# Two cross-attention layers on one core: the second layer's queries in two banks, and queries and keys dealt out anew over the steps

## The chip, the core and the metric

The kernel runs on one NeuronCore of a Trainium2 chip. The core has TensorE (PE in the profile; its weight loads are PEld), VectorE (DVE), ScalarE (ACT), GpSimd (POOL) and SyncE (SP), which only issues DMA transfers here. The metric is the device time of one execution in microseconds (us). Each engine takes its instructions strictly in the order in which the program lists them; an instruction whose operand or buffer is not ready holds up everything behind it on its engine.

## The reference

Input are 64 batches of 256 positions with 320 channels (x), and for each batch 77 context rows of 512 values (73 of text, 4 of an image in the second layer). Both layers have 20 heads of 16 channels. All is float32.

```python
# layer 0: the text path over all 77 rows
q = x @ Wq.T; k = ctx @ Wk.T; v = ctx @ Wv.T          # split into 20 heads
x = softmax(q k^T / 4) v  @ Wo.T + bo + x
# layer 1: 73 text rows, and 4 image rows
q = x @ W_q; k = text @ W_k; v = text @ W_v
probs = softmax(q k^T / 4);  text_out = probs v
qsem = l2norm(probs @ text)                             # 512 values for each head and position
sem = qsem . l2norm(ip)
probs_ip = softmax(q k_ip^T / 4 + 0.5 * sem) * spatial_mask
x = (text_out + probs_ip v_ip) @ W_out + b_out + x
```

In layer 0 the reference's context is cut after 77 rows, so its own image part is over an empty set of rows and adds nothing.

## The kernel before

The kernel keeps channels on the partitions and positions on the free axis. It works on pairs of batches (p = 0 to 31), so that 512 positions are in hand at a time. The 320 channels are held as 2 x 128 ("main") and a rest of 64 ("last"); the rest is stored with batch 0 of the pair on partitions 0 to 63 and batch 1 on partitions 64 to 127.

The attention of one layer and one batch is cut into five units (`UNITS`): two groups of 8 heads times two halves of 128 positions, and one unit with the last 4 heads of both halves. A pair has NU = 10 units. The main loop (line 1050) runs over units g; k = g % 10 is the unit's place in the pair. In step g the kernel handles unit g of layer 0 and unit g - 13 of layer 1, so layer 1 of a pair runs about one pair behind layer 0. A step issues, in this order:

1. `early` and `drains`: what was held from the step before, among it the second part of a projection made in two banks (`held`).
2. on TensorE into the four-bank tile "sc" (one buffer): the `semantics` matmuls of an earlier layer-1 unit (L744, L750), then the scores of both layers (L641).
3. `shifted` on VectorE: maximum and subtraction for each layer (L659, L661).
4. `transposed(1)`: five transposes of layer 1 (L705, L706) into two "tr" tiles, copied out by ScalarE (L712, L713).
5. the exponential of layer 0 on ScalarE (L669), and `weighted` on VectorE (L761, L764).
6. the fillers of the list `first`.
7. `transposed(0)`: the same transposes for layer 0, into two more "tr" tiles, copied out by ScalarE (L731, L732 or L720, L723).
8. the copy of the sums out of "sc" (L1096), the exponential of layer 1 (L672, L673), `normalize` (VectorE L687, L688, POOL L692) and a VectorE reduction (L1107).
9. the fillers of `second`; after the unit u = 1 or u = 4 of layer 0 the attention over the values (`attend`, L777, L782, copied by L801); then the fillers of `third`.

Since "sc" has one buffer, the next step's semantics wait for L1096 of this step, which waits for VectorE. PSUM has two more kinds of tile of a bank each: "tr" with two buffers and "ms" with two. Every filler that multiplies takes "ms" tiles in turn, and its first matmul waits until the tile two before it in the program has been copied out.

The fillers are dealt out by hand, by k, in the function `fillers` (line 941): projections, queries, keys, values, gram matrices and their placements. `keep_order` (line 46) fixes the order of TensorE, ScalarE, VectorE and POOL as the program gives it.

The change touches these fillers: `queries(l, p, m)` makes 128 query channels (m = 0 or 1) of both batches in one bank: two matmuls over 512 columns for the main channels, and two over 256 columns for the last 64 contracted channels, with weights padded by zeros to 128 rows (`wq[l][:, 2 + b]`). For m = 2 it makes the last 64 query channels. `first_queries(p)` makes the first 256 query channels of layer 0 through `halves`: each batch has a bank of its own, eight matmuls over 256 columns for the main channels, and four with only 64 rows for the last channels, one per batch on its own half of the rows. `halves` also serves the output projections `project`. `keys(l, p, i)` makes 128 key channels, `keys_by_head` spreads them by head on POOL.

Layer 1's queries read x after layer 0's `project` and `project_last` have added their results to it (L601, L620 on VectorE).

Of the kernel before, what the change touches and what calls it, by code (L numbers as in the profile page):

```python
# [8 lines left out]
F32 = mybir.dt.float32  # L9
# [9 lines left out]
S = 256  # L19
# [3 lines left out]
P = 128  # L23
# [40 lines left out]
def tile_two_cross_attentions(ctx: ExitStack, tc: tile.TileContext, a: dict, out: bass.AP):  # L64
# [35 lines left out]
    nc = tc.nc  # L100
# [3 lines left out]
    S2 = 2 * S  # L104

    const = ctx.enter_context(tc.tile_pool(name="const", bufs=1))
    big = ctx.enter_context(tc.tile_pool(name="big", bufs=2))
# [5 lines left out]
    pms = ctx.enter_context(tc.tile_pool(name="pms", bufs=2, space=PSUM))  # L113
# [36 lines left out]
    cts, xts = {}, {}  # L150
# [20 lines left out]
    wv, wq, wo, bo = [None] * 2, [None] * 2, [None] * 2, [None] * 2  # L171
# [152 lines left out]
    kTs, kbds, qs, vips, aTs = {}, {}, {}, {}, {}  # L324
# [195 lines left out]
    def halves(name, w, src):  # L520


        main, last = src
        ps = [pms.tile([P, 2, S], F32, tag="ms", name=f"{name}_{b}") for b in range(2)]
        for b in range(2):
            for k in range(2):
                for m in range(2):
                    nc.tensor.matmul(  # L528
                        ps[b][:, m, :], w[:, k, m * P : (m + 1) * P], main[:, k, b * S : (b + 1) * S],
                        start=(k == 0 and m == 0), stop=False,  # L530
                    )

        def rest():
            for m in range(2):
                for b in range(2):
                    rows = slice(b * HALF, (b + 1) * HALF)
                    nc.tensor.matmul(  # L537
                        ps[b][:, m, :], w[rows, 2 + b, m * P : (m + 1) * P], last[rows, :],
                        start=False, stop=(m == 1),
                    )  # L540
            return ps

        return rest

    held = {}

    def queries(l, p, m):

        main, last = xts[p]
        ps = pms.tile([P, 512], F32, tag="ms", name=f"q_ps{l}_{p}_{m}")  # L550
        if m < 2:
            q = qs[l, p, m] = big.tile([P, S2], F32, tag=f"q{l}{m}", name=f"q{l}_{p}_{m}", bufs=1)
            c = slice(m * P, (m + 1) * P)
            for i in range(2):
                nc.tensor.matmul(ps, wq[l][:, i, c], main[:, i, :], start=(i == 0), stop=False)  # L555
            for b in range(2):
                nc.tensor.matmul(ps[:, b * S : (b + 1) * S], wq[l][:, 2 + b, c], last, start=False, stop=(b == 1))  # L557
            nc.scalar.copy(q, ps)
            return
        to = [ps[s * HALF : (s + 1) * HALF, :S].rearrange("p (b t) -> p b t", b=2) for s in range(2)]  # L560
        for i in range(2):
            for s in range(2):
                nc.tensor.matmul(  # L563
                    to[s], wq[l][:, i, C - HALF :],
                    main[:, i, :].rearrange("p (b s t) -> p b s t", b=2, s=2)[:, :, s, :],
                    start=(i == 0), stop=False,
                )
        for b in range(2):
            for s in range(2):
                nc.tensor.matmul(  # L570
                    to[s][:, b, :], wq[l][:, 2 + b, C - HALF :], last[:, s * P : (s + 1) * P],
                    start=False, stop=(b == 1),
                )
        q = qs[l, p, 2] = big.tile([P, 2, P], F32, tag=f"q{l}2", name=f"q{l}_{p}_2", bufs=1)
        nc.scalar.copy(q.rearrange("p b t -> p (b t)"), ps[:, :S])

    def first_queries(p):

        rest = halves(f"q_ps0_{p}", wq[0], xts[p])

        def end():
            ps = rest()
            q = big.tile([P, 2, S2], F32, tag="q0", name=f"q0_{p}")
            for m in range(2):
                qs[0, p, m] = q[:, m, :]
            return [lambda b=b: nc.scalar.copy(q[:, :, b * S : (b + 1) * S], ps[b]) for b in range(2)]  # L586

        held["q"] = end

    def project(l, p):  # L590

# [349 lines left out]
    def fillers(k, p):  # L941


        f = ([], [], [], [])

        def add(half, q, fn, *args):
            if 0 <= q < NP:
                f[half].append((fn, args))

        if k == 0:  # L950
            if p == 0:
                for l in range(2):
                    add(0, p, value_rows, 0, l)
                add(1, p, values, 0, p, 0)
            add(0, p - 1, gram, p - 1, 0)
            add(0, p - 3, project_last, 1, p - 3)
            add(2, p - 2, text_transposed, p - 2, 0)
            if p:
                add(2, p, place_values, 0, p, 0)
            add(2, p - 1, values, 1, p - 1, 0)  # L960
        elif k == 1:
            if p == 0:
                for l in range(2):
                    add(l, p, value_rows, 1, l)
                add(1, p, place_values, 0, p, 0)
            add(0, p, queries, 0, p, 2)
            add(1, p - 1, project, 0, p - 1)
            add(1, p - 1, place_gram, 0)
            add(1, p, keys_by_head, 0, p, 1)
            add(1, p - 1, keys_by_head, 1, p - 1, 0)  # L970
        elif k == 2:
            if p == 0:
                for i in range(2):
                    add(0, p, keys, 1, p, i)
            add(0, p - 1, project_last, 0, p - 1)
            add(1, p + 1, load_x, p + 1)
            add(1, p - 1, queries, 1, p - 1, 0)
            add(1, p - 1, place_values, 1, p - 1, 0)
            add(1, p, values, 0, p, 1)
        elif k == 3:  # L980
            add(0, p + 1, load_context, p + 1)
            add(0, p - 1, queries, 1, p - 1, 2)
            if p == 0:
                add(1, p, image_keys, 0)
            add(1, p - 1, queries, 1, p - 1, 1)
            add(1, p, place_values, 0, p, 1)
            add(1, p - 1, keys_by_head, 1, p - 1, 1)
        elif k == 4:
            if p == 0:
                add(0, p, image_keys, 1)  # L990
            else:
                add(0, p, keys, 1, p, 0)
            add(1, p - 1, values, 1, p - 1, 1)
            add(1, p + 1, first_queries, p + 1)
        elif k == 5:
            if p == 0:
                add(0, p, image_keys, 2)
            add(0, p + 1, keys, 0, p + 1, 0)
            add(2, p - 2, text_transposed, p - 2, 1)
        elif k == 6:  # L1000
            while len(made_rows) * P < min(NB, 2 * (p + 2)) * T:
                rows_todo.extend((len(made_rows), l) for l in range(2))
                made_rows.append(rows_todo[-1])
            for n in range(len(rows_todo) // 2):
                add(0, p, value_rows, *rows_todo.pop(0))
            if p == 0:
                add(0, p, image_norms)
            else:
                add(1, p, keys, 1, p, 1)
            add(1, p - 1, gram, p - 1, 1)  # L1010
            add(1, p, place_image_keys, p)
        elif k == 7:
            add(0, p + 1, keys, 0, p + 1, 1)
            add(1, p + 1, last_keys, p + 1)
            add(1, p - 2, lambda: made.update(wT=image_transposed(p - 2)))
            add(1, p - 1, place_values, 1, p - 1, 1)
            add(1, p - 1, image_values, p - 1, 0)
            if p == 0:
                add(1, p, image_rows)
        elif k == 8:  # L1020
            while rows_todo:
                add(0, p, value_rows, *rows_todo.pop(0))
            add(1, p - 1, place_gram, 1)
            add(1, p + 1, keys_by_head, 0, p + 1, 0)
            add(1, p - 1, image_values, p - 1, 1)
            add(1, p - 2, image_attend_last, p - 2)
            add(3, p - 2, lambda: held.update(i=lambda: image_attend(p - 2)))
        else:
            add(0, p - 2, project, 1, p - 2)
            add(1, p + 1, values, 0, p + 1, 0)  # L1030
            for b in range(2):
                add(1, p - 1, place_image_values, p - 1, b)
        return f
# [7 lines left out]
        keys(0, 0, i)  # L1041
    last_keys(0)
    keys_by_head(0, 0, 0)
    first_queries(0)
    for fn in held.pop("q")():
        fn()

# [2 lines left out]
    for g in range(NP * NU + LAG + 12):  # L1050
        p, k = divmod(g, NU)
# [5 lines left out]
        ps = prod = None  # L1057
# [3 lines left out]
        if now[0] or now[1] or before1:  # L1061
            ps = psc.tile([P, 4, 512], F32, tag="sc", name=f"sc{g}")
# [42 lines left out]
        if before1:  # L1105
            q, b, u = before1[:3]
# [9 lines left out]
        if last0:  # L1116
            q, b, u, _ = last0
# [60 lines left out]
```

## Time and profile before

| | |
|---|---|
| median of 3 runs | 2630.31 us (2629.02 to 2631.37) |
| profiled execution | 2628.61 us, its span 2626.9 us |
| PE busy | 2549.2 us, 97% of the span |
| DVE busy | 1969.9 us, 75% |
| ACT busy | 1538.8 us, 59% |
| POOL busy | 1442.4 us, 55% |
| mean granted TensorE clock | 0.986 |
| unit k = 0 to 9 of one steady pair (from 1249.97 us on) | 8.07, 9.40, 8.62, 7.45, 8.69, 6.43, 6.94, 6.95, 7.51, 7.81 us |
| the pair | 77.87 us |

A float32 matmul of the program stands in the trace as two MATMUL instructions, so a count of x16 is eight matmuls. The end of a matmul is modelled, and the next one of the same kind begins before it; for the time that a group takes, the start of the next group minus its own start is used below. In a timeline a line holds start, duration, engine, line of the program, operation, tiles, tile shape, count, and in brackets the engine's idle time before it and the last of what it waited for.

### The profile page before, as it was taken

The page shows a single profiled execution, that of the slowest core. Times are in us where ns is not written, and L with a number is a line of the kernel's source. Part 1 is how long each engine was busy: PE and PEld are TensorE (multiplying, and loading weights), DVE is VectorE, ACT ScalarE, POOL GpSimd, SP SyncE. Part 2 cuts the span into 40 slices and gives each one's busy share as a digit, 9 for nine tenths or more (in the row PEclk, how much of TensorE's full clock was granted, in tenths as well). Part 3 has the DMA queues.
Part 4 walks back from the last instruction along what each step waited for, and adds up shares of the span by engine and source line. Part 5 has one row for each costly group of instructions (what it writes and reads, how often), then busy time and mean ns, then how long its engine had stood idle before and what let it go on. Part 6 is the DMA issues. An engine that isn't in the chain of part 4 may idle for free.

```text
span 2626.9 us, 73603 instructions
## 1 busy us (share of the span) xinstructions
PE 2549.2 (97%) x26792; PEld 1974.0 (75%) x26792; DVE 1969.9 (75%) x3639; ACT 1538.8 (59%) x3991; POOL 1442.4 (55%) x3515
## 2 busy tenths in 40 slices
PE   7999999999999999999999999999999999999897
PEld 5677777777777777777777777777777777777675
DVE  3577777777777777777777777777777777777864
ACT  3465665655665665665665665655665655665643
POOL 2455555565555565555565555565555565555542
PEclk9999999999999999999999999999999999999986
DMA  5212211112111112111112111112111112111000
GB/s 163 72 29 58 58 42 47 42 51 57 57 44 47 42 51 58 58 42 48 42 52 57 58 42 48 41 52 58 58 42 48 41 52 58 56 38 36 26 22 23
DMA packets 154657, 132.24 MB, mean 50 GB/s; under 512 B 48249, under 2 KB 132985, under 8 KB 154297
## 3 DMA queue, kind: packets, MB, share of 16 engines
q1 hardware_dynamic: 153432, 126.38, 16.8%
q8 instruction: 215, 3.52, 0.5%
q10 hardware_dynamic: 864, 1.15, 0.1%
q14 instruction: 146, 1.19, 0.1%
HBM read 89.53 MB, written 33.91 MB: 47 GB/s over the span
## 4 chain that ended last, share of the span: by engine, by line
PE 87%; DVE 6%; ACT 3%; DMA 1%; issue 1%; POOL 1%; SPq 0%; POOLq 0%; DVEq 0%; ACTq 0%
PE sc L744 13%; PE tr L705 11%; PE o_ps L528 8%; PE sc L641 7%; PE v_ps L379 6%; PE sc L750 5%; PE q_ps L555 4%; PE q_ps L528 4%; PE k_ps L334 4%; PE o_ps L616 3%; PE o_ps L537 3%; PE pv L777 2%; DVE w L661 2%; PE q_ps L557 2%; PE q_ps L563 2%; PE rtr L706 2%
## 5 line engine op out<-in xcount | busy, mean ns | idle before, releaser
L659 DVE TENSOR_REDUCE mx<-sc 128x8 f32<-128x584 f32 (+1 forms) x640 | 497.6, 778 | 460.1 <-PE sc L641 460.0
L692 POOL TENSOR_TENSOR parts<-w,sm 128x512 f32<-128x512 f32 (+1 forms) x640 | 439.6, 708 | 301.6 <-ACT parts L673 180.7
L661 DVE TENSOR_TENSOR w<-sc,mx 128x616 f32<-128x616 f32 x640 | 511.9, 800 | 66.7 <-DVE mx L659 0.5
L712 ACT COPY pt<-tr 128x512 f32<-128x512 f32 x320 | 186.8, 584 | 449.3 <-PE tr L705 437.5
L705 PE MATMUL tr<-ident,parts 128*128 128x128 f32 x2560 | 412.8, 284 | 12.8 <-POOL parts L692 5.2
L744 PEld LDWEIGHTS sc<-gv,pt 64*128 64x128 f32 x5120 | 323.5, 191 | 117.2 <-ACT sums L1096 67.5
L744 PE MATMUL sc<-gv,pt 64*128 64x94 f32 x5120 | 363.3, 282 | 35.1 <-ACT sums L1096 32.7
L705 PEld LDWEIGHTS tr<-ident,parts 128*128 128x128 f32 x2560 | 284.5, 142 | 124.6 <-issue 88.8
L676 POOL COPY att<-w 128x32 f32<-128x32 f32 x320 | 66.8, 209 | 469.7 <-DVE w L661 469.0
L669 ACT ACTIVATE w<-w 128x616 f32<-128x616 f32 x320 | 232.0, 725 | 96.3 <-DVE w L661 95.4
L687 DVE TENSOR_REDUCE sm<-w 128x8 f32<-128x616 f32 x320 | 248.2, 776 | 13.5 <-ACT w L669 13.5
L641 PE MATMUL sc<-kbd,q 32*128 32x154 f32 x5120 | 250.0, 308 | 1.0 <-ACT q L586 0.8
L528 PE MATMUL o_ps<-aT,wo 128*128 128x256 f32 x1024 | 234.3, 383 | 1.6 <-POOL aT L923 1.6
L1107 DVE TENSOR_REDUCE nrm<-prod 128x8 f32<-128x584 f32 x320 | 227.4, 711 | 0.4
L761 DVE TENSOR_TENSOR prod<-sc,parts 128x512 f32<-128x512 f32 x320 | 218.0, 681 | 5.5 <-PE sc L750 5.5
L528 PEld LDWEIGHTS o_ps<-aT,wo 128*128 128x128 f32 x1024 | 192.0, 193 | 25.8 <-POOL aT L923 2.4
L672 ACT ACTIVATE parts<-w 128x512 f32<-128x512 f32 x320 | 206.8, 646 | 0.0
L641 PEld LDWEIGHTS sc<-kbd,q 32*128 32x128 f32 x5120 | 188.5, 188 | 6.0 <-issue 5.0
L731 ACT COPY pt<-tr 128x512 f32<-128x512 f32 x256 | 150.6, 588 | 67.5 <-PE tr L705 66.8
L379 PE MATMUL v_ps<-wv,cf 128*128 128x320 f32 (+1 forms) x624 | 182.1, 438 | 0.0
L706 PE MATMUL rtr<-ident,parts 128*104 128x128 f32 (+1 forms) x640 | 175.9, 275 | 0.0
L1096 ACT COPY sums<-sc 128x168 f32<-128x168 f32 x320 | 96.6, 302 | 118.9 <-DVE prod L764 118.0
(148 smaller groups left out, 4802.9 us busy)
## 6 DMA issues: line engine op xcount, KB each, us to landing
vip<-vip_rows SPq DMA_DIRECT2D x1280, 5.0 KB
out_dram<-x SPq DMA_DIRECT2D x64, 256.0 KB
x<-in_x_dram SPq DMA_DIRECT2D x31, 512.0 KB
v_rows<-vs SPq DMA_DIRECT2D x38, 320.0 KB
vm<-v_rows SPq DMA_DIRECT2D x152, 80.0 KB
ct<-in_ctx_dram SPq DMA_DIRECT2D x32, 308.0 KB
cf<-in_ctx_dram SPq DMA_DIRECT2D x38, 256.0 KB
g_rest<-gram_rest SPq DMA_DIRECT2D x512, 0.5 KB
```

Of the source, the lines that this page charges most:

```text
L379: nc.tensor.matmul(ps[:n, :C], cfs[i][:, k, :n], wv[l][:, k, :], start=(k == 0), stop=(k == KE - 1))
L528: nc.tensor.matmul(ps[b][:, m, :], w[:, k, m * P : (m + 1) * P], main[:, k, b * S : (b + 1) * S], start=(k == 0 and m == 0), stop=False,)
L641: nc.tensor.matmul(ps[:, r, 2 * T * l : 2 * T * (l + 1)], q[rows, b, :] if part == 2 else q[rows, t0 : t0 + P], kbd[rows, part].rearrange( ...
L659: nc.vector.tensor_reduce(mx, sc[:, :, :, :nt], AX.X, ALU.max)
L661: nc.vector.tensor_tensor(w, sc, mx.unsqueeze(3).broadcast_to([P, 4, 2, T]), ALU.subtract)
L669: nc.scalar.activation(w, w, AF.Exp, scale=SCALE)
L687: nc.vector.tensor_reduce(sm, w, AX.X, ALU.add)
L692: nc.gpsimd.tensor_tensor(two[:, 8 * t0 : 8 * t1].rearrange("p (h t) -> p h t", h=8), w[:, :, t0:t1], sm.unsqueeze(2).broadcast_to([P, 8, ...
L705: nc.tensor.transpose(ps[:, i, :], flat[:, i * P : (i + 1) * P], ident)
L706: nc.tensor.transpose(pr[:n, 0, :], flat[:, 4 * P : 4 * P + n], ident)
L744: nc.tensor.matmul(ps[:, i % 2 * 2 + j, at : at + GV], pt[half_rows, i, :], gv[b][half_rows, part, i, :], start=start and i < 2, stop=False,)
L1107: nc.vector.tensor_reduce(eight(stats[q, b][2], u), prod, AX.X, ALU.add)
```

## The change

`first_queries` becomes `queries(l, p)` for both layers. The first 256 query channels of layer 1 are now made by `halves` too: a batch in each of two "ms" banks, the last contracted channels as two row tiles of 64 rows. In layer 0 the second part is still held over to the next step; in layer 1 the second part and the two copies follow at once. The tile of layer 1's queries is one tile "q1" with one buffer instead of two tiles. The last 64 query channels keep their form, in a function of their own, `last_queries`.

The fillers are dealt out anew:

- the last queries of layer 0: from k = 1, first list, to k = 3, second list
- the first 256 queries of layer 1: from k = 2 and k = 3 (a half in the second list of each) to k = 2, third list, that is after the attention
- `keys_by_head` of layer 1, batch 1: from k = 3 to k = 2, second list, ahead of `place_values`
- the first half of layer 1's keys (p > 0): from k = 4, first list, to k = 3, second list

```diff
-    def queries(l, p, m):
+    def last_queries(l, p):
 
         main, last = xts[p]
-        ps = pms.tile([P, 512], F32, tag="ms", name=f"q_ps{l}_{p}_{m}")
-        if m < 2:
-            q = qs[l, p, m] = big.tile([P, S2], F32, tag=f"q{l}{m}", name=f"q{l}_{p}_{m}", bufs=1)
-            c = slice(m * P, (m + 1) * P)
-            for i in range(2):
-                nc.tensor.matmul(ps, wq[l][:, i, c], main[:, i, :], start=(i == 0), stop=False)
-            for b in range(2):
-                nc.tensor.matmul(ps[:, b * S : (b + 1) * S], wq[l][:, 2 + b, c], last, start=False, stop=(b == 1))
-            nc.scalar.copy(q, ps)
-            return
+        ps = pms.tile([P, 512], F32, tag="ms", name=f"q_ps{l}_{p}_2")
...
-    def first_queries(p):
+    def queries(l, p):
 
-        rest = halves(f"q_ps0_{p}", wq[0], xts[p])
+        rest = halves(f"q_ps{l}_{p}", wq[l], xts[p])
 
         def end():
             ps = rest()
-            q = big.tile([P, 2, S2], F32, tag="q0", name=f"q0_{p}")
+            q = big.tile([P, 2, S2], F32, tag=f"q{l}", name=f"q{l}_{p}", bufs=2 - l)
             for m in range(2):
-                qs[0, p, m] = q[:, m, :]
+                qs[l, p, m] = q[:, m, :]
             return [lambda b=b: nc.scalar.copy(q[:, :, b * S : (b + 1) * S], ps[b]) for b in range(2)]
 
-        held["q"] = end
+        if l:
+            for fn in end():
+                fn()
+        else:
+            held["q"] = end
...
         elif k == 1:
...
-            add(0, p, queries, 0, p, 2)
             add(1, p - 1, project, 0, p - 1)
...
         elif k == 2:
...
-            add(1, p - 1, queries, 1, p - 1, 0)
+            add(1, p - 1, keys_by_head, 1, p - 1, 1)
             add(1, p - 1, place_values, 1, p - 1, 0)
             add(1, p, values, 0, p, 1)
+            add(2, p - 1, queries, 1, p - 1)
         elif k == 3:
             add(0, p + 1, load_context, p + 1)
-            add(0, p - 1, queries, 1, p - 1, 2)
+            add(0, p - 1, last_queries, 1, p - 1)
             if p == 0:
                 add(1, p, image_keys, 0)
-            add(1, p - 1, queries, 1, p - 1, 1)
+            if p:
+                add(1, p, keys, 1, p, 0)
+            add(1, p, last_queries, 0, p)
             add(1, p, place_values, 0, p, 1)
-            add(1, p - 1, keys_by_head, 1, p - 1, 1)
         elif k == 4:
             if p == 0:
                 add(0, p, image_keys, 1)
-            else:
-                add(0, p, keys, 1, p, 0)
             add(1, p - 1, values, 1, p - 1, 1)
-            add(1, p + 1, first_queries, p + 1)
+            add(1, p + 1, queries, 0, p + 1)
```

More of the change, by code (lines that the diff above doesn't have):

```diff
@@ L1043, in tile_two_cross_attentions @@
     keys_by_head(0, 0, 0)
-    first_queries(0)
+    queries(0, 0)
     for fn in held.pop("q")():
```

## The prediction

> **What bounds the kernel now.** I read the page's busy shares first, then the timeline of one steady pair (units g = 160 to 165), cut into its units by the first semantic matmul (L744) of each, then places where the trace already shows what the change will make. The page's first part:
>
> ```profile
> PE 2549.2 (97%) x26792; PEld 1974.0 (75%) x26792; DVE 1969.9 (75%) x3639; ACT 1538.8 (59%) x3991; POOL 1442.4 (55%) x3515
> ```
>
> TensorE is nearly always busy, so one would price this change by TensorE time alone. The windows of units k = 1, 2, 3, 4 (stretch, its length, busy time per engine, granted clock) say the same: hardly any idle TensorE time in any of the four.
>
> ```profile
> 1258.04:1267.44 9.40, 9.34 (x91) 7.65 (x92) 6.48 (x13) 4.36 (x15) 5.74 (x10) 1.00 0.17 41
> 1267.44:1276.06 8.62, 8.61 (x89) 5.24 (x85) 7.39 (x14) 3.80 (x9) 4.66 (x12) 1.00 0.29 89
> 1276.06:1283.51 7.45, 7.45 (x79) 5.24 (x75) 5.02 (x9) 3.77 (x10) 3.76 (x18) 1.00 0.14 40
> 1283.51:1292.20 8.69, 8.69 (x84) 7.67 (x85) 6.47 (x12) 5.30 (x12) 5.72 (x11) 1.00 0.09 26
> ```
>
> But TensorE works in program order, and between two sets of transposes it depends on ScalarE: there are two "tr" banks, each unit takes four tiles from them, so the transposes of layer 0 (second L705 of a unit) write the bank that the transposes of layer 1 wrote, and must wait until ScalarE has copied it out (L712). What lies between the two, the fillers of the first list, hides that. Timeline of k = 1, TensorE and then ScalarE (start, duration, instruction):
>
> ```profile
> 1260.77 1.08 PE L563 MATMUL q_ps<-x,wq 128*64 128x256 f32 x8
> 1261.68 0.61 PE L570 MATMUL q_ps<-x,wq 128*64 128x128 f32 x8
> 1262.35 0.63 PE L705 MATMUL tr<-ident,parts 128*128 128x128 f32 x4
> ...
> 1261.40 0.34 ACT L882 ACTIVATE num<-num 128x160 f32<-128x160 f32 x1 [2.50 <-POOL num L879]
> 1261.64 0.57 ACT L712 COPY pt<-tr 128x512 f32<-128x512 f32 x1
> ```
>
> L712 ends at 1262.21 and the transposes begin 0.14 later, with TensorE already idle for 0.07 us (1261.68 + 0.61 = 1262.29). The last layer-0 queries (L563, L570) thus fill exactly the time of that copy, which is late here because ScalarE first does L882, which waits for POOL. The end of the run has units with an empty first list (here g = 317):
>
> ```profile
> 2487.58 0.27 PE L706 MATMUL rtr<-ident,parts 128*128 128x128 f32 x1
> 2488.56 0.63 PE L705 MATMUL tr<-ident,parts 128*128 128x128 f32 x4 [0.71 <-POOL iw L839]
> ...
> 2487.83 0.59 ACT L712 COPY pt<-tr 128x512 f32<-128x512 f32 x1 [1.80 <-PE tr L705]
> ```
>
> The copy ends at 2488.42, the transposes start 0.14 later, and TensorE idles 0.71 us (the POOL instruction named is merely the last of several waits).
>
> **The change, part by part, per pair of batches.**
>
> *k = 1 loses the last layer-0 queries.* 1262.35 - 1260.77 = 1.58 us of TensorE work go, but the transposes still cannot start before L712's end plus 0.14, that is 1262.35. L882 waits for POOL's L879, which no part of the change moves. Gain: 0.00; a 1.5 us stall stands where the work stood. Bounds: 0.0 to 0.1.
>
> *k = 2 loses one half of the layer-1 queries (second list), gains all of them (third list, after the attention).* The places now:
>
> ```profile
> 1272.10 1.88 PE L555 MATMUL q_ps<-x,wq 128*128 128x512 f32 x4
> 1273.99 1.13 PE L557 MATMUL q_ps<-x,wq 128*128 128x256 f32 x4
> 1275.06 0.64 PE L777 MATMUL pv<-pt,v 128*32 128x256 f32 x8
> ...
> 1272.19 0.58 ACT L731 COPY pt<-tr 128x512 f32<-128x512 f32 x1 [0.18 <-PE tr L705]
> ...
> 1273.46 0.47 DVE L620 SCALAR_TENSOR_TENSOR x<-o_ps,bo,x 128x256 f32<-128x256 f32 x1
> ```
>
> The old half takes 1275.06 - 1272.10 = 2.96 us, the attention 1276.06 - 1275.06 = 1.00. The queries stand between the transposes and the attention (L777), which reads ScalarE's copy L731. Without them the attention is next in the order, at 1272.10, but the copy ends at 1272.77. Unit g = 2 at the start has just this order:
>
> ```profile
> 34.09 0.27 PE L706 MATMUL rtr<-ident,parts 128*104 128x128 f32 x1
> ...
> 34.40 0.60 ACT L731 COPY pt<-tr 128x512 f32<-128x512 f32 x1
> ...
> 35.14 0.64 PE L777 MATMUL pv<-pt,v 128*32 128x256 f32 x8 [0.78 <-POOL kbd L365]
> ```
>
> There TensorE idles 0.78 us and starts 0.14 after the copy. So the attention runs from 1272.91 to 1273.91. The queries then need two "ms" banks; the first is the one project_last used, free when VectorE's L620 ends (1273.93), and today L557, which needs the same instruction, starts 0.06 after it: 1273.99. The second is the attention's own, freed by its copy (L801): ScalarE finishes L673 at 1274.58 and needs 0.37, long before the 1.8 us of the first bank's matmuls are over. How long the new form takes is shown by layer 0, which has it already, in k = 4:
>
> ```profile
> 1287.68 3.62 PE L528 MATMUL q_ps<-x,wq 128*128 128x256 f32 x16
> 1291.23 1.14 PE L537 MATMUL q_ps<-x,wq 64*128 64x256 f32 x8
> ...
> 1286.28 0.59 ACT L712 COPY pt<-tr 128x512 f32<-128x512 f32 x1 [2.08 <-PE tr L705]
> ```
>
> From 1287.68 to the next unit at 1292.20: 4.52 us. k = 2 would end at 1273.99 + 4.52 = 1278.51 instead of 1276.06: +2.45. Bounds: +1.56 (4.52 - 2.96, no stall) and +2.65 (0.1 more at either start).
>
> *k = 3 loses the other half, gains the layer-1 keys and the last layer-0 queries.* Lost: 1283.51 - 1280.83 (start of L555 there) = 2.68. Gained: keys (L334, 8 matmuls) 1287.13 - 1286.13 = 1.00, and the last queries 1280.23 - 1278.78 = 1.45. Where the next matmul has the same tile shape it starts 0.16 before the modelled end of the one before (keys: 1286.13 + 1.16 = 1287.29 against 1287.13), with another shape 0.07 (L570: 1279.69 + 0.61 = 1280.30 against 1280.23); keys to column-tiled queries is such a seam, +0.09. Net -0.14, bounds -0.25 and +0.1. [...]
>
> *k = 4 loses the keys.* They are 1.00 us between the two sets of transposes. L712 ends at 1286.87; plus 0.14 the transposes can start at 1287.01 instead of 1287.13. Gain: 0.12; bounds 0.0 and 0.2.
>
> *Copies and POOL.* ScalarE still makes two copies of 512 columns for these queries. They now both start when the last row-tiled matmul ends, 0.17 us into k = 3, with ScalarE free (its last instruction of k = 2 ends at 1274.95, over 3 us earlier), and take 1.06 us together (as L586 does). The first reader, layer 1's scores, comes 1.33 + 0.35 = 1.68 us into k = 3 (1277.39 - 1276.06, and half of the scores' 0.69): nothing. Neither keys nor queries issue a DMA. keys_by_head of layer 1 (0.70 + 0.44 us on POOL) moves a unit forward, ahead of twelve small place_values instructions in k = 2; POOL idles 1.82 us after these today (1281.66), and the unit is 2.45 us longer. SP's fetch of layer-0 values waits for place_values to free "vm" and so issues some 1.1 us later; its reader on POOL (1284.71) follows k = 3's L692 and moves back by 2.45. Nothing.
>
> Sum per pair: 0.00 + 2.45 - 0.14 - 0.12 = +2.19 us. The first pair runs without layer 1 and the last without layer 0; I leave their differences (about 1.5 us either way) out and count 31 pairs: +67.9 us. The profiled execution took 2628.61 (span 2626.9 and 1.7 around it), hence 2696.5; it lies 1.7 below the median of the runs, 2630.31, so 2698.
>
> **Rivals.**
>
> *Work alone decides (faster).* If the transposes in k = 1 and k = 4 did not wait for L712, both units would shrink by their whole work: -1.58 + 1.56 - 0.14 - 1.00 = -1.16 us, or 36 us: 2594. For it: the shares of 97%. Against it: the 0.14 us from copy to transposes, the same in k = 1 and at g = 317. It decides once these two units give back 2.31 of their 2.58 us.
>
> *No stall before the attention.* k = 2 grows by 1.56 only: +1.30 per pair, 40 us, 2671. Against it: the 0.78 us at g = 2.
>
> *The new copies come late.* If they stood behind ScalarE's two exponentials (0.90 us), layer 1's scores in k = 3 would wait some 0.6 us more: +19 us, 2717. Against it: ScalarE is idle there.
>
> *The stalls lower the clock.* From 2540 to 2560 the granted clock is 0.50. If 1.5 us per pair were lost that way, +46 us: 2744. Against it: from 2480 to 2490 TensorE is busy 7.15 of 10 us and the clock stays 1.00.
>
> **How the numbers follow.** Forecast 0.80; work alone 0.04; no stall 0.07; late copies 0.06; clock 0.03. The forecast's own bounds (the ends above, summed: -1.2 to +0.6 us per pair, hardly all at once; half of each is likely) give 2680 to 2707; I reach from 2678 to 2716, near the late copies, and leave out the rest. A measurement of this kernel tells 0.2% (5 us) from no change. Faster is the first rival, 0.04; 0.01 for the same; 0.95 slower.
>
> **What the profile after would show.** k = 1 as long as now (9.40), with about 1.5 us of TensorE idle before the second transposes, put down to L712 or what waits beside it; k = 4 about 8.57 with 0.8 us idle there; k = 2 about 11.07, with 0.7 idle before the attention; k = 3 about 7.3. TensorE's busy time falls though the span grows. The prediction is wrong if k = 1 shrinks by over 0.3 us, if k = 2 grows by less than 2, or if layer 1's scores in k = 3 wait for the query copies.

## The result: 2.8% slower

The changed kernel takes 2704.73 us in the median of five runs (2697.01 to 2708.21), the kernel before 2630.31 (2623.28 to 2631.73): a ratio of 1.0281, 95% interval 1.0268 to 1.0294. The forecast was 2698, with 2678 to 2716 as the range. The profiled execution took 2702.18 us, its span 2700.5.

The first part of the page after:

```profile
PE 2535.2 (94%) x27048; PEld 2006.2 (74%) x27048; DVE 1970.4 (73%) x3639; ACT 1537.2 (57%) x3991; POOL 1442.1 (53%) x3515
```

TensorE is busy for 14 us less (2549.2 before) and the span is 73.6 us longer. The windows of k = 1 to 4 of the same pair as before (g = 161 to 164; stretch, length, busy time of PE, PEld, DVE, ACT, POOL, granted clock, DMA share, GB/s) show where:

```profile
1296.45:1305.84 9.39, 7.89 (x76) 6.64 (x77) 6.48 (x13) 4.20 (x14) 5.71 (x10) 1.00 0.19 40
1305.84:1317.00 11.16, 10.51 (x104) 7.73 (x102) 7.39 (x14) 3.48 (x9) 7.16 (x21) 1.00 0.24 70
1317.00:1324.22 7.22, 7.22 (x93) 5.72 (x89) 4.89 (x9) 4.57 (x12) 2.21 (x11) 1.00 0.16 39
1324.22:1332.81 8.59, 7.88 (x76) 6.63 (x76) 6.50 (x12) 4.88 (x12) 4.72 (x9) 1.00 0.12 26
```

k = 1 lost 1.45 us of TensorE's busy time and 0.01 us of its length: 9.39 against 9.40, with 1.50 us in which TensorE idles. k = 4 lost 0.81 us of busy time and 0.10 of its length. k = 2 grew by 2.54 us, 0.65 of it idle time. k = 3 shrank by 0.23. The other six steps of the pair are as they were, to 0.01 us.

The line numbers have moved: L712 is now L707, L705 is L700, L731 is L726, L777 is L772, L620 is L615, L744 is L739, L882 is L877, L1096 is L1090. The timeline of k = 1, TensorE and then ScalarE:

```profile
1298.97 0.27 PE L701 MATMUL rtr<-ident,parts 128*128 128x128 f32 x1
1300.75 0.63 PE L700 MATMUL tr<-ident,parts 128*128 128x128 f32 x4 [1.50 <-ACT pt L707]
...
1299.79 0.34 ACT L877 ACTIVATE num<-num 128x160 f32<-128x160 f32 x1 [2.48 <-POOL num L874]
1300.04 0.57 ACT L707 COPY pt<-tr 128x512 f32<-128x512 f32 x1
```

Nothing stands between the two sets of transposes any more. ScalarE sits in front of L877 for POOL, its copy ends at 1300.61, and the second transposes begin 0.14 us later, as they did before with the queries in between. In k = 2 the attention and the queries stand as follows (TensorE, ScalarE, VectorE):

```profile
1310.39 0.27 PE L701 MATMUL rtr<-ident,parts 128*104 128x128 f32 x1
1311.23 0.64 PE L772 MATMUL pv<-pt,v 128*32 128x256 f32 x8 [0.56 <-ACT pt L726]
1312.39 3.72 PE L528 MATMUL q_ps<-x,wq 128*128 128x256 f32 x16
1316.04 1.14 PE L537 MATMUL q_ps<-x,wq 64*128 64x256 f32 x8
...
1310.59 0.58 ACT L726 COPY pt<-tr 128x512 f32<-128x512 f32 x1 [0.18 <-PE tr L700]
...
1311.86 0.48 DVE L615 SCALAR_TENSOR_TENSOR x<-o_ps,bo,x 128x256 f32<-128x256 f32 x1
```

The attention waits for L726 (ends at 1311.17), the queries for L615 (ends at 1312.34), then they run for 4.61 us. In k = 4 the transposes wait too:

```profile
1327.72 0.63 PE L700 MATMUL tr<-ident,parts 128*128 128x128 f32 x4 [0.71 <-ACT pt L707]
```

The waits of TensorE, after (us in total, times, longest us; the last line is one of its weight loads):

```profile
PE tr L700 <- ACT pt L707: 68.9, 63, 2.1
PE sc L739 <- ACT sums L1090: 34.8, 70, 2.4
PE pv L772 <- ACT pt L726: 18.8, 32, 1.1
...
PEld q_ps L528 <- DVE x L615: 17.0, 30, 0.6
```

and the first of these before:

```profile
PE tr L705 <- ACT pt L712: 4.3, 5, 1.5
```

The wait for the copy of the first transposes comes 63 times instead of 5, and 59 of these are in k = 1 and k = 4, once each in nearly every pair. The wait of the attention for its copy is new in the steady pairs and comes once in each.

### The profile page after: what moved, and what is told of

The parts are those of the page before. It is cut to its first block, busy times and chain, and to the rows that moved or that the text cites. A ratio compares the mean times of both kernels' runs of the same rounds, so it can differ in the third digit from the quotient of the medians.

```text
span 2700.5 us, 74170 instructions
## 1 busy us (share of the span) xinstructions
PE 2535.2 (94%) x27048; PEld 2006.2 (74%) x27048; DVE 1970.4 (73%) x3639; ACT 1537.2 (57%) x3991; POOL 1442.1 (53%) x3515
## 4 chain that ended last, share of the span: by engine, by line
PE 63%; DVE 13%; POOL 7%; ACT 5%; issue 4%; SPq 4%; DMA 4%; POOLq 0%; DVEq 0%; ACTq 0%
PE sc L739 9%; PE q_ps L528 8%; PE tr L700 7%; PE sc L636 5%; PE o_ps L528 5%; PE v_ps L379 5%; DVE w L656 4%; PE sc L745 3%; DVE mx L654 3%; PE k_ps L334 3%; PE q_ps L537 2%; PE q_ps L554 2%; DVE prod L756 2%; POOL parts L687 2%; SPq L395 2%
## 5 line engine op out<-in xcount | busy, mean ns | idle before, releaser
L700 PE MATMUL tr<-ident,parts 128*128 128x128 f32 x2560 | 415.7, 286 | 76.8 <-ACT pt L707 68.9
L707 ACT COPY pt<-tr 128x512 f32<-128x512 f32 x320 | 186.8, 584 | 430.9 <-PE tr L700 428.4
L700 PEld LDWEIGHTS tr<-ident,parts 128*128 128x128 f32 x2560 | 284.3, 142 | 195.6 <-issue 73.8
L739 PEld LDWEIGHTS sc<-gv,pt 64*128 64x128 f32 x5120 | 324.0, 190 | 103.0 <-ACT sums L1090 69.6
L739 PE MATMUL sc<-gv,pt 64*128 64x94 f32 x5120 | 358.2, 280 | 37.2 <-ACT sums L1090 34.8
L528 PE MATMUL q_ps<-x,wq 128*128 128x256 f32 x1024 | 234.9, 382 | 2.5
L528 PEld LDWEIGHTS q_ps<-x,wq 128*128 128x128 f32 x1024 | 189.4, 190 | 40.9 <-DVE x L615 17.0
L726 ACT COPY pt<-tr 128x512 f32<-128x512 f32 x256 | 149.3, 583 | 68.9 <-PE tr L700 67.6
```

The source lines that it names most:

```text
L528: nc.tensor.matmul(ps[b][:, m, :], w[:, k, m * P : (m + 1) * P], main[:, k, b * S : (b + 1) * S], start=(k == 0 and m == 0), stop=False,)
L700: nc.tensor.transpose(ps[:, i, :], flat[:, i * P : (i + 1) * P], ident)
L739: nc.tensor.matmul(ps[:, i % 2 * 2 + j, at : at + GV], pt[half_rows, i, :], gv[b][half_rows, part, i, :], start=start and i < 2, stop=False,)
```

## The experiments

Theory: a unit's second transposes start when ScalarE has copied the first out, not when TensorE is free, and the attention of k = 2 likewise waits for its copy. Work in front of these points is free up to the wait's length, and taking it away gains nothing. Rivals: TensorE's work alone decides; the new form with two banks and row tiles costs the time; the dealing of the two moved fillers costs all of it. Each ratio below is to the kernel before as timed beside that run (2629.71 or 2632.19 us in the median).

### TensorE work taken away in k = 1, nothing moved

```diff
-            add(0, p, queries, 0, p, 2)
+            if p == 0:
+                add(0, p, queries, 0, p, 2)
...
-        q, kbd, t0 = qs[l, p, part], kbds[l, b], b * S + s * P
+        q, kbd, t0 = qs[l, p if l or part < 2 else 0, part], kbds[l, b], b * S + s * P
```

> The kernel before, and the last 64 query channels of layer 0 are made for the first pair only and used for all pairs: 31 times 1.58 us of TensorE work are left out of k = 1, nothing is moved. Copy-wait theory: the second transposes of k = 1 still begin 0.14 us after the copy L712, so k = 1 stays at 9.4 us and the time at 2630 (2626 to 2640). Work-alone rival: 1.5 us less per pair, 2583.

Measured: 2635.70 us, a ratio of 1.0025 (1.0016 to 1.0034) to the kernel before. This kernel leaves out the last layer-0 queries of all pairs but the first, and with them their 31 copies on ScalarE. TensorE's busy time fell from 2549.2 to 2510.6 us and the time rose by a quarter of a per cent. The median of k = 1 over the pairs is 9.39 us. Its timeline:

```profile
1267.26 0.63 PE L705 MATMUL tr<-ident,parts 128*128 128x128 f32 x4 [1.52 <-ACT pt L712]
...
1266.55 0.57 ACT L712 COPY pt<-tr 128x512 f32<-128x512 f32 x1
```

The copy ends at 1267.12, the transposes start at 1267.26. The work of the last layer-0 queries was free where it stood; work alone, which asked for 2583, is out. That it got even slower probably belongs to the clock, below: the steady part of this trace has three half-clock stretches, worth 5.1 us of full clock. No run tests this apart.

### What makes the copy late

```diff
         if k == 0:
...
-            if p:
-                add(2, p, place_values, 0, p, 0)
-            add(2, p - 1, values, 1, p - 1, 0)
         elif k == 1:
...
+            if p:
+                add(3, p, place_values, 0, p, 0)
+            add(3, p - 1, values, 1, p - 1, 0)
```

> The changed kernel, and POOL does layer 0's place_values of batch 0 (1.7 us) at the start of k = 1, behind the image subtraction, instead of at the end of k = 0, ahead of it; the fetch of layer 1's values follows it. TensorE's program is the same. Copy-wait theory with POOL as the first cause: ScalarE's image exponential in k = 1 is released earlier, its copy of the layer-1 transposes ends at 3.36 us into k = 1 instead of 4.16, the second transposes begin at 3.5 instead of 4.31, k = 1 goes from 9.40 to 8.6 us, and the time from 2704 to about 2680. Rival (the stall in k = 1 is TensorE's own, or that of a bank of the fillers): unchanged, 2704.

Measured: 2673.82 us, 1.0167 (1.0151 to 1.0182) of the kernel before, 30.9 us less than the changed kernel; TensorE's order is that of the changed kernel. k = 1 takes 8.54 us. Its copy and its second transposes:

```profile
1282.78 0.59 ACT L707 COPY pt<-tr 128x512 f32<-128x512 f32 x1 [0.66 <-PE tr L700]
...
1283.51 0.63 PE L700 MATMUL tr<-ident,parts 128*128 128x128 f32 x4 [0.66 <-POOL vr L464]
```

The copy now waits for TensorE and no longer for ScalarE's image exponential, ends at 1283.37, and the transposes follow 0.14 us later. The instruction of POOL that the line names ended at the same moment (1283.37), and is not what they read. Over 29 pairs of this trace the transposes begin 0.14 us after the copy, to 0.001 us, and between 0.12 and 0.14 us after that instruction, so it is the copy that they follow. So three engines make the stall: POOL does layer 0's values first, ScalarE waits for POOL in front of the copy, TensorE for the copy.

The same move in the kernel before:

> The kernel before with POOL's place_values moved as in pool_later, nothing else. Copy-wait theory: the last layer-0 queries stand in k = 1 and already cover the late copy but for 0.1 us, so the earlier copy gains at most 0.13 us per pair: 2626 (2622 to 2631). Rival (the move helps by itself, through POOL): 25 us less as in pool_later, 2605.

Measured: 2626.18 us, 0.9983 (0.9969 to 0.9996). k = 1 went from 9.40 to

```profile
1257.29:1266.58 9.29, 9.29 (x92) 7.62 (x93) 6.47 (x13) 4.67 (x15) 5.64 (x10) 1.00 0.15 36
```

The move is worth 0.85 us per pair where the stall is open, and 0.11 where the queries cover it.

### The old form at the new place

```diff
     def queries(l, p):
 
+        if l:
+            main, last = xts[p]
+            for m in range(2):
...
+                for i in range(2):
+                    nc.tensor.matmul(ps, wq[l][:, i, c], main[:, i, :], start=(i == 0), stop=False)
+                for b in range(2):
+                    nc.tensor.matmul(ps[:, b * S : (b + 1) * S], wq[l][:, 2 + b, c], last, start=False, stop=(b == 1))
+                nc.scalar.copy(q, ps)
+            return
         rest = halves(f"q_ps{l}_{p}", wq[l], xts[p])
```

> The changed kernel with the old form of layer 1's 256 query channels (two banks of 128 channels by 512 columns, weights padded with zeros) at the new place after the attention in k = 2; all moves stay. Copy-wait theory: the new form itself saves time, 5.36 us against 4.52 per pair, so k = 2 goes from 11.17 to 12.0 and the time from 2704 to about 2731. Form rival (a batch in each of two banks and the two row tiles are what costs the time): back towards 2630, at least below 2690.

Measured: 2735.79 us, 1.0405 (1.0388 to 1.0423). k = 2 and k = 3:

```profile
1319.96:1331.87 11.91, 11.27 (x97) 6.86 (x93) 7.39 (x14) 4.06 (x10) 7.76 (x24) 1.00 0.26 69
1331.87:1339.18 7.31, 7.31 (x91) 5.82 (x90) 4.88 (x9) 4.08 (x11) 1.61 (x7) 1.00 0.15 38
```

Against 11.16 and 7.22 with the new form: 0.84 us per pair, which is twice the 2.68 us that a half takes in k = 3 of the kernel before, less the 4.52 us of the new form. A batch in each bank with row tiles does save TensorE that time. The change is thus a gain of 0.84 us per pair by the form and a loss of 3.05 by the moves (2.21 in all).

### Two of the moves undone

```diff
         elif k == 1:
+            add(0, p, last_queries, 0, p)
...
         elif k == 3:
...
-            if p:
-                add(1, p, keys, 1, p, 0)
-            add(1, p, last_queries, 0, p)
...
         elif k == 4:
+            else:
+                add(0, p, keys, 1, p, 0)
```

> The changed kernel with two of its moves undone: the last layer-0 queries back in the first list of k = 1, layer 1's keys back in the first list of k = 4. TensorE's work is the same, only its place differs. Copy-wait theory (what stands between two sets of transposes is hidden behind ScalarE's copy of the first set): k = 1 stays at 9.4 us though 1.5 us of work are put in; k = 4 goes from 8.5 to 8.6; k = 3 loses 2.45 us of work but can't go below what the copy of the sums allows, about 6.6 (from 7.2). Per pair -0.5 us, over 31 pairs -16 us: about 2688. Work-alone rival: the same work, so the same time, 2704. Dealing-is-all rival (the slowdown comes only from those two moves): near 2630.

Measured: 2705.52 us, 1.0291 (1.0275 to 1.0307), where the theory had asked for 2688. The steps in a pair are what it said, though: k = 1 9.39 us, k = 2 11.16, and k = 3 and 4

```profile
1319.60:1326.09 6.49, 4.83 (x68) 3.69 (x65) 4.19 (x7) 3.83 (x10) 2.20 (x10) 1.00 0.19 43
1326.09:1334.78 8.69, 8.69 (x83) 7.65 (x85) 7.29 (x14) 5.36 (x13) 4.79 (x9) 1.00 0.11 26
```

against 7.22 and 8.59: -0.63 per pair, some -20 us. But this is an undisturbed pair. In the median over the pairs k = 4 takes 10.24 us. k = 3 now ends with 1.65 us in which TensorE waits for the copy of the sums, and after it the trace shows, in many pairs, a stretch like the second of these two:

```profile
1161.30:1164.70 3.40, 1.74 (x25) 1.32 (x22) 3.23 (x7) 2.65 (x7) 0.21 (x1) 1.00 0.06 14
1164.80:1168.20 3.40, 3.40 (x37) 2.92 (x35) 1.27 (x3) 0.00 (x0) 2.92 (x5) 0.50 0.05 9
```

The granted clock is half for about 3.4 us. Between 160 and 2480 us the clock record of this trace has 16 such stretches, together 61.4 us, worth some 31 us of full clock; the changed kernel has two in that time (6.8 us), the kernel before none. That took back what the better dealing gave. The time alone would fit the rival that TensorE's work decides (the same work, 2704); the lengths of the steps do not. The rival that the two moved fillers cost everything, near 2630, is out. The half clock was the clock rival of the forecast, in a kernel where I did not expect it.

### More work against the half clock

To see whether the idle time causes these stretches, useless work is put into it:

```diff
         elif k == 3:
...
+            add(1, p, last_queries, 0, p)
```

> covers_back, and layer 0's last queries are made a second time in the second list of k = 3: 1.45 us of useless TensorE work and one copy per pair, put into the 1.65 us in which TensorE waits for the copy of the sums at the end of k = 3. Clock theory (covers_back missed its forecast because TensorE, idle for 1.65 us in one stretch there, is granted half its clock in the following 3.4 us in about 18 of 31 pairs, 1.6 us each): k = 3 stays at 6.5 us, the half-clock stretches in k = 4 go, and the time falls by about 25 us to some 2685 (2678 to 2692). Rival (the longer k = 4 comes from the keys back in its first list): unchanged, 2705. Work-alone rival: 45 us more, 2750.

Measured: 2683.31 us, 1.0205 (1.0183 to 1.0226). With 1.45 us more of work in each pair the kernel is 22 us faster than without it. Not one half-clock stretch is left between 160 and 2480 us, and k = 4 takes 8.68 us in the median:

```profile
1306.44:1312.93 6.49, 6.29 (x84) 4.69 (x80) 4.19 (x7) 3.84 (x10) 2.23 (x10) 1.00 0.19 43
1312.93:1321.62 8.69, 8.69 (x83) 7.65 (x85) 7.29 (x14) 5.62 (x14) 4.79 (x9) 1.00 0.10 26
```

k = 3 has the same length and 1.46 us more of it is busy. So the keys in k = 4 are not the cause, and the idle time is; and work alone, which asked for 2750 here, is out again.

### The attention moved, and a version that beats both

On top of the kernel with two moves undone, the attention of k = 2 goes to k = 3, where there is room, and the queries follow the transposes directly:

```diff
-            if u == 1 or u == len(UNITS) - 1:
-                attend(q, b, int(u > 1))
+            if u == 2 - b or u == len(UNITS) - 1:
+                attend(q, b, int(u == len(UNITS) - 1))
```

> covers_back, and layer 0's attention of the first batch's first eight-head group is done in k = 3 instead of k = 2, so that the layer-1 queries follow the transposes of k = 2 directly. Copy-wait theory: the 0.65 us stall before the attention goes and its 1.0 us of work move into the idle time of k = 3: k = 2 from 11.17 to about 9.4, k = 3 stays at 6.5 with about 0.7 us idle, too little for half-clock stretches. Per pair against the kernel before: k = 2 +0.75, k = 3 -0.96, together -0.2: about 2622 (2615 to 2632). Rival (the stall only moves to the queries' second bank, which waits for VectorE's addition in project_last): k = 2 no shorter than 10.2, 2650 or more.

Measured: 2621.03 us, 0.9970 (0.9955 to 0.9984). k = 2 and k = 3:

```profile
1265.81:1275.25 9.44, 9.44 (x88) 7.22 (x86) 7.39 (x14) 3.21 (x8) 5.50 (x14) 1.00 0.28 84
1275.25:1281.74 6.49, 5.84 (x85) 4.12 (x81) 4.20 (x7) 3.84 (x10) 3.89 (x17) 1.00 0.17 41
```

k = 2 gives up 1.72 us, and k = 3 takes the attention in without growing. Part of the wait did move to the queries' second bank, which needs VectorE's L615:

```profile
1270.48 3.88 PE L528 MATMUL q_ps<-x,wq 128*128 128x256 f32 x16
1274.29 1.13 PE L537 MATMUL q_ps<-x,wq 64*128 64x256 f32 x8
...
PEld q_ps L528 <- DVE x L615: 11.8, 30, 0.4
```

The queries take 4.77 us (1270.48 to 1275.25) against the 4.52 of layer 0. These 0.25 us per pair are still open, but k = 2 is far from the 10.2 us of the rival.

The last kernel adds the move of POOL's values and fills the rest of k = 3 with transposes from k = 0:

```diff
         if k == 0:
...
-            add(2, p - 2, text_transposed, p - 2, 0)
...
         elif k == 3:
...
+            add(2, p - 2, text_transposed, p - 2, 0)
```

> attend_later with two more moves: POOL's place_values as in pool_later, and the transposes of layer 1's text output of the first batch (0.77 us of TensorE, four ScalarE copies) from the end of k = 0 to the end of k = 3, into its idle time. Theory: k = 0 from 8.07 to 7.3, k = 1 keeps 9.3, since its cover takes as long as now but the copy is no longer late; k = 3 stays near 6.5: about -0.85 us per pair more than attend_later, 2595 (2588 to 2610), faster than both kernels by over 1%. Rival (the four copies on ScalarE at the end of k = 3 delay the copies of the transposes in k = 4, and k = 4 gives back what k = 0 gains): 2620.

Measured: 2603.10 us, 0.9896 (0.9876 to 0.9917), 1.0% faster than the kernel before and 3.8% faster than the changed one. Its steps k = 0, 1, 2, 3:

```profile
1237.99:1245.26 7.27, 7.27 (x112) 5.37 (x110) 6.87 (x15) 6.71 (x16) 5.63 (x14) 1.00 0.27 88
1245.26:1254.55 9.29, 9.29 (x94) 7.63 (x92) 7.24 (x15) 4.35 (x12) 6.36 (x12) 1.00 0.13 32
1254.55:1263.99 9.44, 9.44 (x88) 7.22 (x86) 7.39 (x14) 3.22 (x8) 5.61 (x14) 1.00 0.35 93
1263.99:1270.56 6.57, 6.57 (x90) 4.72 (x86) 4.28 (x7) 3.92 (x10) 3.90 (x17) 1.00 0.15 40
```

k = 0 fell from 8.07 to 7.27 and k = 3 is now busy throughout, 0.08 us longer than the 6.49 that it took with TensorE waiting for the copy of the sums. By this the new form of the queries is worth having once every place that loses work has a use for the time. That is argued and not shown: no run has the old form in this order (by the 0.84 us per pair above it would be some 26 us slower, an estimate), and of these moves the kernel before was tried with POOL's alone.

## Why the prediction was right

- *k = 1, gain 0.00.* Measured 0.01. The step that carried it, that the second transposes start 0.14 us after the copy whatever stands in front of them, holds in both kernels, in the kernel with work left out, and, with the copy moved earlier, in the one with POOL's order changed: 0.143 to 0.146 us in 30 pairs of each of the four traces.
- *k = 2, +2.45.* Measured +2.54. The attention began 0.06 after its copy and not 0.14, which gained nothing, since the queries after it wait for VectorE; the queries began 0.05 after VectorE's addition, as said; and they took 4.61 us instead of the 4.52 that layer 0's took, nearly all of it in the full-array part (3.65 against 3.55 us): its first instruction, which follows a wait here, takes 0.32 us to the next instead of 0.22.
- *k = 3, -0.14.* Measured -0.23. The keys with their seam took 1.09 us and the last queries 1.45, as summed. The missing 0.09 is a seam I had not counted: k = 3 begins with the 64-row semantic matmuls, which now follow 64-row matmuls instead of column-tiled ones; they hold 1.03 us where they held 1.13 (1276.06 before, 1317.00 after).
- *k = 4, -0.12.* Measured -0.10.
- *Copies and POOL, nothing.* ScalarE's two copies came 0.20 us into k = 3 and took 1.07 us; neither the scores nor anything on POOL waited for them in the steady pairs.
- *The sum.* +2.19 per pair forecast, +2.20 measured over these four steps (80.08 us for the pair after, 77.87 before). That the sum came out to 0.01 us is luck: the 0.09 too little in k = 2 and the 0.09 too much in k = 3 cancel. Thirty pairs at 2.21 are 66 us of the 73.6 by which the span grew. The rest is in terms that I had left out or taken for steady. The start cost 4.9: the first semantic matmul starts at 116.85 us instead of 111.98. Of this the first ten steps, with layer 0 alone, lost 2.1; the forecast had put the first pair at 1.5 either way. In the second pair, where layer 1 only begins, k = 1 did gain 1.3, having no layer 1 to wait for, but k = 2 lost 3.3, k = 3 lost 1.0 and k = 4 gained 0.15. Two half-clock stretches (at 892.6 and 974.6 us) cost 1.67 us each. I had given the clock a chance of 0.03 as a rival worth 46 us; it came as a surcharge of some 3.

What the forecast said of the rivals stands: work alone is shown wrong by the kernel with work left out, and no stall before the attention by the 0.56 us in the timeline. The late copies did not come.

## What to carry to other kernels

Look at what a filler covers before it is moved: an engine that is 97% busy, as TensorE here, can still be paced by a copy on another engine, and the sign is a constant distance (here 0.14 us) between the end of that copy and the start of the next work, with the filler ending just there. Work that stands in such a place is free up to the length of the wait (here 1.50 us in k = 1), and moving it into a step that is really full costs its whole length (here 1.09 and 1.45 us in k = 3). When a leaner form frees time (here 0.84 us per pair), find the step that can use it first, or the time turns into idle stretches, and these can lower the clock of TensorE on top (here to 0.50 for about 3.4 us at a time).

## What the hardware showed that I had not expected

In the steady part of the changed kernel TensorE lost half its clock twice after standing still for 1.5 us. The starts of the ten half-clock stretches in its clock record lie whole multiples of 3.4133 us apart, to 0.003 us, and the stall of k = 1 falls in different places of this grid. Three stretches on the grid, each with the one after it:

```profile
889.20:892.60 3.40, 1.94 (x35) 1.45 (x33) 2.05 (x3) 0.91 (x5) 2.47 (x6) 1.00 0.01 1
892.60:896.00 3.40, 3.35 (x11) 2.90 (x12) 3.26 (x8) 2.40 (x7) 0.66 (x2) 0.51 0.09 22
971.20:974.60 3.40, 1.88 (x33) 1.51 (x32) 2.27 (x3) 1.14 (x4) 2.23 (x5) 1.00 0.01 1
974.60:978.00 3.40, 3.40 (x12) 2.87 (x11) 3.29 (x7) 2.20 (x6) 0.91 (x2) 0.50 0.21 50
1053.10:1056.50 3.40, 1.89 (x32) 1.52 (x33) 2.32 (x4) 1.28 (x4) 2.09 (x5) 1.00 0.01 1
1056.50:1059.90 3.40, 3.40 (x19) 3.04 (x18) 3.33 (x8) 2.06 (x6) 1.03 (x2) 1.00 0.03 5
```

With TensorE busy for 1.88 to 1.94 us of 3.40 the clock of the next stretch was halved twice and left alone once; with 1.74 us, in the kernel with two moves undone, it was halved. The clock record of these traces gives each half-clock stretch of the steady part as 3.413 us or a multiple of it, and the two here start 81.92 us apart, 24 times 3.4133. Matmul ends are modelled, so I can't say at which share the clock gives way. The traces show half clock after some of the idle stretches of 1.5 to 1.65 us, and none with stalls up to 0.71 us: the kernel with POOL's order changed, whose longest stall in the steady pairs is the 0.71 us of k = 4, shows no half-clock stretch between 160 and 2480 us.

The number of these stretches may differ between executions of one kernel. The runs of the changed kernel spread over 11 us, and their mean granted clock goes from 0.987 for the fastest (2697.01 us) to 0.982 for the slowest (2708.21 us). But the kernel before spreads as far (2622.68 us at 0.990 to 2637.91 at 0.983) with no such stretch in the steady part of its one trace (there they come before 150 us and from 2539 us on), so the start and the end of a run may do it as well. Only one execution of each kernel has a trace, so this stays open.
